# Second projection of a graph-attention layer as seven products of half blocks: six single accumulator banks and three softmax buffers

## The chip, the cores and the metric

The kernel runs on one core of one Trainium2 chip. The metric is the device time of one execution in microseconds.

## The reference

A batch of 32 graphs with 512 nodes and 512 features goes through a layer norm with ReLU and two graph-attention layers, and the input is added at the end. Cut to what matters:

```python
def gat_layer(x, mask, W, a_src, a_dst, bias, concat):
    xl = (x @ W).reshape(B, N, H, F)                   # projection
    e = leaky_relu(asrc[:, :, None, :] + adst[:, None, :, :], 0.2)
    attn = softmax(where(mask, e, -1e9), axis=1)
    out = einsum('bsdh,bshf->bdhf', attn, xl)          # gather
    ...
h = elu(gat_layer(h, mask, W1, ..., b1, concat=True))  # 4 heads of 256
h = gat_layer(h, mask, W2, ..., b2, concat=False)      # 1 head of 512: W2 is 1024 x 512
out = x + h
```

## The kernel before

One loop step works on three batches at once. TensorE's order is written by hand: first projection and first gather of batch i+1, second projection of batch i, second gather of batch i-1. The compiler orders the other engines. The softmax runs on VectorE and ScalarE between these stages; its row terms are transposed by TensorE (`prr`), copied by VectorE (`rrr`), written to DRAM (`drr`) and read back to all partitions (`orr`).

The second projection is plain: 4 tiles of rows, 8 slices of the contraction, two halves of columns, and per tile a pair of banks of PSUM, the memory in which TensorE's sums build up. The two attention columns of W2 ride along, one at each end.

```python
def project2(b):
    h1 = H1.pop(b)
    v = x2(b)
    for t in range(NT):
        ps = psum.tile([P, 2, 512], F32, tag="mm", name=f"pxm{b}_{t}", bufs=3)
        for k in range(FT):
            for j in range(2):
                nc.tensor.matmul(
                    ps[:, j, : W - 1], h1[:, k, t * P : (t + 1) * P],
                    w2_sb[:, k, j * (W - 1) : (j + 1) * (W - 1)],
                    start=(k == 0), stop=(k == FT - 1),
                )
            ...
        nc.scalar.activation(
            v[:, t, :].rearrange("p (c w) -> p c w", c=2), ps[:, :, : W - 1], AF.Copy
        )
```

## Time and profile before

| | before |
|---|---|
| time, median of 3 runs | 3347.83 us (3346.74 to 3349.3) |
| TensorE busy | 3244.2 us, 97% |
| VectorE, ScalarE busy | 64%, 52% |
| TensorE idle: start, middle, tail | 54.4, 26.8, 15.5 us |
| half clock after 215 us and before the tail | none |

The last two rows are sums over the trace: start is the first 215 us, tail the last 165 us (idle time up to TensorE's last matmul), middle what lies between. TensorE's granted clock is recorded in windows: 12 in the trace of this kernel, each at 1.0 or at 0.5 of full clock. A busy TensorE with little idle time means that taking work from it should pay, as long as nothing else comes late.

Two groups of the page that the prediction did not use; columns are operation, operands, count, busy us, mean ns, idle time before:

```profile
L235 DVE CUSTOM_DVE_ANT_0 l<-l,mt 128x512 f32<-128x512 f32 x640 | 532.9, 861 | 499.2 <-ACT l L232 498.2
L360 POOL TENSOR_TENSOR xr<-xr,b_sb 128x1024 f32<-128x1024 f32 x64 | 194.9, 3046 | 2818.6 <-DMA xr<-in_x_dram 2450.4
```

The median of the first group is 690 ns. A mean of 861 says that a few of the 640 are far longer: 55 of them take 2.7 us on average.

### The profile page before, as it was taken

What the parts mean: (1) busy time and instruction counts of PE and PEld (TensorE: products, weight loads), DVE (VectorE), ACT (ScalarE), POOL (GpSimd) and SP (SyncE); (2) the same over time, 40 slices, a digit from 0 to 9 for tenths busy, and PEclk for the clock granted to TensorE, in tenths of its full rate; (3) what the DMA queues carried; (4) which work ended last, traced back from release to release, by engine and by line L of the source; (5) the groups of instructions that cost most, each with busy time, mean ns of one, the idle gap of its engine ahead of it and who ended that gap; (6) DMA issues with size and microseconds to landing.
All of it is one profiled execution on the core that took longest, in us unless ns stands there. A gap on an engine that the chain in (4) does not pass through costs nothing.

```text
span 3345.9 us, 35756 instructions
## 1 busy us (share of the span) xinstructions
PE 3244.2 (97%) x12544; PEld 2221.7 (66%) x12544; DVE 2128.6 (64%) x4675; ACT 1748.3 (52%) x3489; POOL 228.3 (7%) x102
## 2 busy tenths in 40 slices
PE   4999999999999999999999999999999999999997
PEld 3666676676676666776666766766766667667664
DVE  6567666666666566666676665666665766666663
ACT  3555555545555445555455554455554555554551
POOL 0000000000000000000000000000000000000000
PEclk8999999999999999999999999999999999999998
DMA  5112222222222122222122221222221222221111
GB/s 186 46 60 79 92 95 79 70 76 79 92 91 74 63 81 84 95 83 81 62 79 92 95 79 64 83 78 91 91 76 57 82 89 95 80 71 62 67 67 54
DMA packets 120389, 269.41 MB, mean 81 GB/s; under 512 B 15504, under 2 KB 20496, under 8 KB 120208
## 3 DMA queue, kind: packets, MB, share of 16 engines
q1 hardware_dynamic: 120208, 267.12, 23.7%
q8 instruction: 98, 1.61, 0.2%
q14 instruction: 83, 0.68, 0.1%
HBM read 232.53 MB, written 34.54 MB: 80 GB/s over the span
## 4 chain that ended last, share of the span: by engine, by line
PE 67%; DVE 18%; DMA 8%; ACT 4%; issue 1%; POOL 1%; SPq 0%; POOLq 0%; ACTq 0%; DVEq 0%
PE po L301 26%; PE pxl L282 20%; PE pxm L334 10%; PE po L366 9%; DVE p L261 5%; DVE l L235 5%; DVE p L269 3%; DMA oas<-das 2%; DMA x<-in_x_dram 2%; ACT l L232 2%; ACT l L239 2%; DMA orr<-drr 2%; DMA das<-ras 1%; DVE hn L151 1%; DMA adj<-in_adj_dram 1%
## 5 line engine op out<-in xcount | busy, mean ns | idle before, releaser
L282 PE MATMUL pxl<-w_sb,ht 128*128 128x258 f32 x4096 | 933.5, 384 | 2.4 <-DVE j L101 2.4
L334 PE MATMUL pxm<-w_sb,h 128*128 128x257 f32 x4096 | 922.4, 379 | 0.0
L301 PE MATMUL po<-p,xl 128*128 128x512 f32 x2048 | 891.1, 594 | 0.0
L282 PEld LDWEIGHTS pxl<-w_sb,ht 128*128 128x128 f32 x4096 | 768.5, 191 | 126.8 <-issue 11.5
L235 DVE CUSTOM_DVE_ANT_0 l<-l,mt 128x512 f32<-128x512 f32 x640 | 532.9, 861 | 499.2 <-ACT l L232 498.2
L334 PEld LDWEIGHTS pxm<-w_sb,h 128*128 128x128 f32 x4096 | 761.6, 190 | 126.0 <-issue 10.4
L301 PEld LDWEIGHTS po<-p,xl 128*128 128x128 f32 x2048 | 388.0, 191 | 474.2 <-issue 454.6
L265 ACT ACTIVATE p<-p,lo 128x512 f32<-128x512 f32 x640 | 429.2, 716 | 471.0 <-DVE p L261 470.5
L232 ACT ACTIVATE l<-oas,sc 128x512 f32<-128x512 f32 x640 | 427.1, 710 | 211.7 <-DMA oas<-das 211.7
L239 ACT ACTIVATE l<-l,low 128x512 f32<-128x512 f32 x640 | 454.3, 711 | 130.2 <-DVE low L235 129.7
L261 DVE SCALAR_TENSOR_TENSOR p<-orr,lo 128x512 f32<-128x512 f32 x640 | 444.7, 749 | 82.2 <-DMA orr<-drr 82.0
L366 PE MATMUL po<-xl,p 128*128 128x512 f32 x1024 | 459.3, 595 | 14.6 <-DVE p L269 14.6
L269 DVE TENSOR_TENSOR p<-p,m 128x1024 f32<-128x1024 f32 x320 | 385.9, 1224 | 2.9 <-ACT p L265 2.9
L360 POOL TENSOR_TENSOR xr<-xr,b_sb 128x1024 f32<-128x1024 f32 x64 | 194.9, 3046 | 2818.6 <-DMA xr<-in_x_dram 2450.4
L286 ACT ACTIVATE xl<-pxl 128x516 f32<-128x516 f32 x256 | 149.0, 594 | 416.9 <-PE pxl L282 416.6
L366 PEld LDWEIGHTS po<-xl,p 128*128 128x128 f32 x1024 | 188.0, 191 | 225.8 <-issue 223.8
L311 ACT ACTIVATE e<-po,b_sb 128x512 f32<-128x512 f32 x256 | 171.3, 681 | 297.7 <-PE po L301 152.8
L312 DVE TENSOR_SCALAR e<-e 128x512 f32<-128x512 f32 x256 | 108.7, 425 | 172.5 <-ACT e L311 172.1
L313 DVE SCALAR_TENSOR_TENSOR h<-po,b_sb,e 128x512 f32<-128x512 f32 x256 | 192.1, 751 | 14.7
L142 DVE BATCH_NORM_STATS2 stats<-x 128x6 f32<-128x512 f32 x128 | 87.7, 686 | 95.4 <-DMA x<-in_x_dram 94.9
L239 ACT ACTIVATION_READ_ACCUMULATOR l<-l,low 128x1 f32 x640 | 120.5, 188 | 0.0
L180 DVE TENSOR_SCALAR mt<-pm 128x512 bf16<-128x512 bf16 x128 | 53.3, 417 | 104.5 <-PE pm L177 103.8
(43 smaller groups left out, 1066.7 us busy)
## 6 DMA issues: line engine op xcount, KB each, us to landing
orr<-drr SPq DMA_DIRECT2D x160, 512.0 KB
x<-in_x_dram SPq DMA_DIRECT2D x128, 256.0 KB
adj<-in_adj_dram SPq DMA_DIRECT2D x128, 256.0 KB
xr<-in_x_dram SPq DMA_DIRECT2D x128, 256.0 KB
oas<-das SPq DMA_DIRECT2D x64, 512.0 KB
out_dram<-xr SPq DMA_DIRECT2D x128, 256.0 KB
oas<-das SPq DMA_DIRECT2D x32, 256.0 KB
drr<-rrr SPq DMA_DIRECT2D x160, 4.0 KB
```

Of the source, the lines that this page charges most:

```text
L232: nc.scalar.activation(e, self.asr[i][:, j, :], AF.Prelu, bias=ad[:, d : d + 1], alpha=SLOPE)
L235: nc.vector.tensor_tensor_reduce(out=e, in0=e, in1=MASKT[self.b][:, d, :], scale=-1.0, scalar=BIG, op0=OP.add, op1=OP.min, accum_out=low[: ...
L239: nc.scalar.activation(e, e, AF.Exp, bias=low[:, d : d + 1], scale=-1.0, accum_out=tot[:, d : d + 1])
L261: nc.vector.scalar_tensor_tensor(p[:, u, :], rr[:, 0, :], lo[:, 0, j, u : u + 1], rr[:, 1, :], op0=OP.add, op1=OP.max,)
L265: nc.scalar.activation(p[:, u, :], p[:, u, :], AF.Exp, bias=lo[:, 1, j, u : u + 1])
L269: nc.vector.tensor_tensor(pp, pp, MASK[self.b][:, t : t + 2, :], op=OP.min)
L282: nc.tensor.matmul(ps[:, j, :W], ht[:, k, t * P : (t + 1) * P], w1_sb[:, k, hp + j, :], start=(k == 0), stop=(k == KT - 1),)
L301: nc.tensor.matmul(ps[:, f, :], xl[:, s, h, 2 + f * P : 2 + (f + 1) * P], p[:, s, :], start=(s == 0), stop=(s == NT - 1),)
L313: nc.vector.scalar_tensor_tensor(H1[b][:, g, :], ps[:, f, :], bias, e, op0=OP.add, op1=OP.max)
L334: nc.tensor.matmul(ps[:, j, : W - 1], h1[:, k, t * P : (t + 1) * P], w2_sb[:, k, j * (W - 1) : (j + 1) * (W - 1)], start=(k == 0), stop=(k ...
L360: nc.gpsimd.tensor_tensor(xr, xr, b2_sb[:, None, :].to_broadcast([P, 2, D]), op=OP.add)
L366: nc.tensor.matmul(ps[:, j, :], p[:, s, (d + j) * P : (d + j + 1) * P], v[:, s, 1 : DO + 1], start=(s == 0), stop=(s == NT - 1),)
```

## The change

The intent is to save TensorE time. With seven block products in place of eight (the Winograd form of Strassen's scheme), the two halves of rows, contraction and columns need 56 matmuls instead of 64. The price: sums of blocks of h1 (`sums2`) and of W2 (once), an evaluation in which several products build up in one bank and are read in between, and SBUF (on-chip memory) space. So the pairs of banks become six single banks, the softmax weights get three buffers instead of four, the score tiles three instead of four, and the normalised rows overwrite x. The core of the diff, cut:

```diff
-    w2_sb = const.tile([P, FT, DO + 2], F32, name="w2_sb")
+    w2_sb = const.tile([P, 7, KH, W2H], F32, name="w2_sb")
...
-            p = work.tile([P, NT, N], F32, tag="p", name=f"p{self.b}_{self.layer}_{h}", bufs=4)
+            p = work.tile([P, NT, N], F32, tag="p", name=f"p{self.b}_{self.layer}_{h}", bufs=3)
...
+    def sums2(b):
+        ...
+        nc.vector.tensor_add(s1, a21, a22)
+        nc.vector.tensor_sub(a21, a11, a21)
+        nc.vector.tensor_sub(s2, s1, a11)
+        nc.vector.tensor_sub(s4, a12, s2)
+        LEFT[b] = {1: a11, 2: a12, 3: s4, 4: a22, 5: s1, 6: s2, 7: a21}
...
     def project2(b):
+        def product(m, n, acc, first):
+            if first:
+                bank[m, acc] = psum.tile([P, 512], F32, tag="mm", name=f"pxm{b}_{m}{acc}", bufs=6)
+            ps = bank[m, acc]
+            for k in range(KH):
+                nc.tensor.matmul(
+                    ps[:, :W2H], left[n][:, k, m * P : (m + 1) * P], RIGHT[n][:, k, :],
+                    start=(first and k == 0), stop=(k == KH - 1), skip_group_check=True,
+                )
...
+        for m, n in (
+            (0, 1), (0, 2), (0, 5), (1, 1), (0, 6), (1, 2), (1, 5),
+            (0, 7), (1, 6), (0, 3), (1, 7), (0, 4), (1, 3), (1, 4),
+        ):
+            acc = {1: "a", 2: "g", 5: "b", 6: "a", 7: "a", 3: "b", 4: "a"}[n]
+            product(m, n, acc, n in (1, 2, 5))
+            ...
+            if n in (1, 5, 6):      # ScalarE copies the bank out; the bank goes on
+                nc.scalar.activation(block(*to, m), ps, AF.Copy)
+            elif n == 4:
+                nc.scalar.activation(block(1, 0, m), ps, AF.Copy)
+            else:                   # 2, 7, 3: VectorE adds the bank to a block
+                nc.vector.tensor_add(to, ps, to)
...
-            stages.insert(0 if last else 1, project2(i))
+            order = [g2] * 4 + [c2] * 14
+            if last:
+                order = [g2] * 2 + [c2] * 14 + [g2] * 2
```

Bank "a" of row block m takes product 1, is copied out, takes product 6 on top, is copied out, takes 7, is added to a block, and takes 4. Before each of these steps the program makes TensorE wait for the read of the step before (such waits for ScalarE's copies come to 93 us in the profile after). "(1, 7)" below means product 7 of row block 1.

## The prediction

> **What bounds the kernel now.** I read the busy shares first, then the costliest groups, the waits of TensorE, a table by stage, and at last the order of events inside one batch. The busy shares, the granted clock and the costliest TensorE groups of the page:
>
> ```profile
> PE 3244.2 (97%) x12544; PEld 2221.7 (66%) x12544; DVE 2128.6 (64%) x4675; ACT 1748.3 (52%) x3489; POOL 228.3 (7%) x102
> ...
> PEclk8999999999999999999999999999999999999998
> ...
> L282 PE MATMUL pxl<-w_sb,ht 128*128 128x258 f32 x4096 | 933.5, 384 | 2.4 <-DVE j L101 2.4
> L334 PE MATMUL pxm<-w_sb,h 128*128 128x257 f32 x4096 | 922.4, 379 | 0.0
> ```
>
> TensorE is the bound: 97% busy, at full clock after the start. The second projection (L334) has 4096 records for 32 batches, 128 per batch; the code issues 4 x 8 x 2 = 64 matmuls per batch, so each f32 matmul is two records. The mean of 379 ns holds pipeline overlap. The price is the distance of starts, from the TensorE timeline of the second projection of one middle batch:
>
> ```profile
> 1582.68 3.64 PE L334 MATMUL pxm<-w_sb,h 128*128 128x257 f32 x16
> 1586.15 0.60 PE L156 MATMUL pht<-identf,hn 128*128 128x128 f32 x4
> 1586.59 3.64 PE L334 MATMUL pxm<-w_sb,h 128*128 128x257 f32 x16
> 1590.07 0.27 PE L196 MATMUL prr<-identf,r 128*8 128x128 f32 x1
> 1590.18 3.64 PE L334 MATMUL pxm<-w_sb,h 128*128 128x257 f32 x16
> ...
> 1606.04 0.27 PE L196 MATMUL prr<-identf,r 128*8 128x128 f32 x1 [0.79 <-DVE rrr L198]
> ```
>
> 16 records take 1586.15 - 1582.68 = 3.47 us: **217 ns each**. The one steady gap is the last line: the transpose of head 3's row terms waits for a VectorE copy that frees its PSUM buffer. The waits of TensorE over the whole run (columns: total us, times, longest us):
>
> ```profile
> PE prr L196 <- DVE rrr L198: 26.2, 27, 1.8
> PE prr L196 <- DVE r L246: 20.1, 4, 7.3
> PE po L366 <- DVE p L269: 14.6, 1, 14.6
> PE pht L156 <- DVE hn L151: 10.0, 2, 9.4
> ```
>
> The first is the steady gap, 0.8 to 0.9 us per batch; the others are the start and the tail. So TensorE sets the time, but with no room: the softmax chain of VectorE, ScalarE and DMA arrives 0.8 us late per batch. The table by stage of that batch (first projection, second gather, second projection, first gather):
>
> ```profile
> 1539.10:1568.30 29.20, 29.20 (x148) 25.15 (x147) 13.64 (x31) 11.24 (x20) 0.00 (x0) 1.00 0.22 73
> 1568.30:1582.70 14.40, 14.40 (x40) 6.45 (x39) 9.00 (x31) 12.69 (x31) 0.00 (x0) 1.00 0.36 113
> 1582.70:1613.10 30.40, 29.61 (x144) 25.34 (x143) 24.13 (x45) 15.28 (x33) 7.66 (x3) 1.00 0.35 121
> 1613.10:1640.70 27.60, 27.60 (x67) 12.18 (x66) 19.39 (x40) 15.11 (x28) 0.00 (x0) 1.00 0.10 29
> ```
>
> Columns are the stretch, its us, then busy us of PE, weight load, DVE, ACT, POOL. VectorE is at 24.1 of 30.4 us in the second projection and 19.4 of 27.6 in the first gather, but only 13.6 of 29.2 in the first projection.
>
> [...] from 1598.7 to 1602.7 ScalarE idles for VectorE's p while the eviction of a finished projection tile waits behind it.
>
> **The change part by part.**
>
> Removed: a batch goes from 64 to 14 x 4 = 56 matmuls of 257 columns (the attention columns ride along, one in each half). That is 16 records x 217 ns = 3.47 us a batch, **111.1 us** over 32.
>
> Added on VectorE per batch: four sums of 128x1024, about 1.13 us each start to start[...]: 4.5 us. They stand in the first projection, where VectorE has 15 us free, and are needed 14 us of second gather later: hidden. Six additions of a finished product from PSUM, 257 columns, 0.4 us each: 2.4 us, inside the crowded stage. Four gather additions of 512 for two of 1024: +0.4 us. VectorE goes to about 73 of 98 us: still no bound by sum. ScalarE's evictions become half as wide and twice as many: 1 us more at most. Both hidden by sum.
>
> At the start: the attention columns of W2 take 32 reductions of 256 columns at 0.35 us (start distance of L101) instead of 16 of 512 at 0.61 (L116): +1.4; four small adds 0.6; four subtractions of the half blocks of 1028 columns, 4.5. VectorE's queue holds TensorE up there (waits for m and mt), so about **+6 us**. In the first batch the second projection no longer stands in front of its first softmax transposes: the four empty turns of the gather pass at once, about **+5 us**.
>
> At the tail: before, after the last first gather TensorE ran the whole second projection at once (from 3266.97), and only then needed the weights of the batch before, ready at 3277.8. Now two gather steps come first and must wait for these weights: 11 us, up to 15 if the sums get ahead of them, say 13. After the projection the gather that hides the last softmax is half as long, and the rows' transpose comes one gather step later. From the end of the first gather to the last gather: before 3324.6 - 3267 = 57.6 us; after about 13 + 6.9 + 24.3 + 3.4 + 28.6 (the measured way from 3296.0 to 3324.6) = 76.2. That is +18.6, and as the 3.5 us saved are already counted, **+22 us**.
>
> Six single banks for three pairs: the same PSUM. Three softmax buffers for four: head 3's weights wait until head 0's gather ends, 7 us into the first gather; they are needed at 20.6 us and take about 7: hidden. Row normalising in place: hidden.
>
> **The steady term, where I choose.** Before, eviction of a projection tile started on average 2.5, 5.0, 1.0 and 5.0 us after its last matmul (mean over 32 batches, computed from the trace), and it did not matter, since three pairs of banks were there. Now a later product accumulates on the same bank, so TensorE must wait for the read in between. The distance is three products (5.2 us) for block one, two (3.5) for the next, and for the second row block's 6 to 7 only one, 1.7 us; the final reuse of the first bank has 3.5. Also, the transposes of heads 2 and 3 are now three products (5.2 us) apart where they were two half tiles (6.9), and the copy between them is the one that is already late. Against that, the compiler's order of VectorE and ScalarE will be another one, and a stall of TensorE gives the chain time. I take 1.2 us more than the present gap per batch, **+36 us** over 30 batches.
>
> Sum: 3347.8 - 111.1 + 6 + 5 + 22 + 36 = **3306 us**.
>
> **The rivals.** (1) The saving arrives whole but for the ends: steady term zero, 3270 us, or 3245 if the finer banks also close the present gap. For it: VectorE and ScalarE have idle time, and the order of products is interleaved with care. Against: the chain is late already and gets 2.8 us more VectorE work in its stage. (2) A new wait takes the place: evictions behind blocked queue heads stall TensorE about 3 us a batch, giving 3360. For it: latencies of 5 us against distances of 1.7 to 3.5. Against: the compiler orders the evictions anew, and one stall gives the later ones time. (3) VectorE becomes the bound: against it, 73 of 98 us. (4) The DMA queue: 24% of its engines' time, and no transfer grows: no change.
>
> **Range and chances.** A steady term of -0.6 to +2.9 us a batch round 3270 gives 3252 to 3357. Faster by over 2% means under 3281, a steady term under 0.4 us: 0.30. Slower by over 2% means over 3415, a term near 5 us: 0.08. Within 2%: 0.62.
>
> **What would show each step.** The second projection's records should fall to 3584 at an unchanged start distance of 217 ns; otherwise the saving is mis-sized. The waits of TensorE should list the projection's products waiting for ScalarE's copy or VectorE's addition, and the prr wait, together about 2 us a batch; if they total under 0.9, rival one holds, and if over 4, rival two. A wait of 11 to 15 us of the second gather should stand before the last projection, and the last wait for p should be near 22 us; if either is missing the tail term is wrong. A wait of the first product for the sums would show that they are not hidden. The prediction is wrong most easily by the order of the two in-order queues, which I cannot see.

3347.8 - 111.1 + 6 + 5 + 22 + 36 is 3305.7. The 1.13 us of a sum: in the profile before, the next instruction starts 1.135 us after a mask minimum of this size (median of 283). What the profile after shows for the new work of VectorE: 1.20 to 1.23 us for a sum of h1, the four of a batch together 5.4 us where 4.5 were given; 0.40 to 0.42 us for the addition of a product; 2.7 us a batch for the four gather additions, 2.4 for the two before; 1.20 to 1.22 us for each of the four subtractions of 1028 columns.

## More of the kernel before

The line of GpSimd is untouched by the change, and it will matter:

```python
def gather2(b):
    for d in range(0, NT, 2):
        xr = work.tile([P, 2, D], F32, tag="xr", name=f"xr{b}_{d}", bufs=2)
        ...  # two loads of x
        nc.gpsimd.tensor_tensor(xr, xr, b2_sb[:, None, :].to_broadcast([P, 2, D]), op=OP.add)
        ...  # matmuls into ps
        nc.vector.tensor_tensor(xr, ps, xr, op=OP.add)
        ...  # stores
```

In the second gather GpSimd adds the bias to the residual rows ahead of time, and VectorE adds the gathered sum.

## The result and the profile after

| | before | after |
|---|---|---|
| median of four fast runs | 3348.28 us | 3376.72 us (3373.38 to 3383.01) |
| ratio after to before | | 1.0088, interval 1.007 to 1.0105 |
| TensorE matmul records | 12544 | 12032 |
| TensorE busy, profiled run | 3244.2 us | 3184.9 us |
| TensorE idle: start, middle, tail | 54.4, 26.8, 15.5 us | 59.3, 91.6, 31.9 us |
| half-clock windows in the middle | 0 | 22, together 92.2 us |

A ratio is the mean time of one kernel's fast runs over that of the other's of the same rounds, so it is not quite the ratio of the medians. The change made the kernel 0.9% slower, outside the range of 3252 to 3357 us.

The busy shares and the clock of the page after:

```profile
PE 3184.9 (94%) x12032; PEld 2158.0 (64%) x12032; DVE 2324.9 (69%) x5099; ACT 1791.2 (53%) x3873; POOL 218.9 (6%) x102
...
PEclk8899999999999999999999999999999999999998
```

There are exactly 512 records fewer, 32 x 16, and they should take away 111.1 us. TensorE's busy time fell by 59.3 us only; the other 51.8 us are matmuls that ran slower. The strip of the clock hides this, since most half-clock windows in the middle (3.4 us) are short against a slice of 84 us; the mean granted clock shows it, 0.973 after 0.989. The waits of TensorE over the run:

```profile
PE pxm_1a L381 <- ACT xl L399: 88.3, 30, 4.4
PE prr L227 <- DVE r L277: 31.8, 6, 12.0
PE po L427 <- DVE p L300: 19.8, 2, 10.6
```

The 26 us for the transposes are gone. In their place (1, 7) waits for ScalarE's copy of (1, 6) out of their common bank, 2.9 us a time. The TensorE timeline of one batch:

```profile
1494.27 1.90 PE L381 MATMUL pxm_1a<-w_sb,hs 128*128 128x257 f32 x8
1496.01 0.27 PE L227 MATMUL prr<-identf,r 128*8 128x128 f32 x1
1496.11 1.91 PE L381 MATMUL pxm_0b<-w_sb,hs 128*128 128x257 f32 x8
1497.86 0.60 PE L187 MATMUL pht<-identf,x 128*128 128x128 f32 x4
1502.40 3.62 PE L381 MATMUL pxm_1a<-w_sb,h 128*128 128x257 f32 x8 [3.94 <-ACT xl L399]
1505.85 1.90 PE L381 MATMUL pxm_0a<-w_sb,h 128*128 128x257 f32 x8
```

(1, 6) ends at 1496.0. One product stands between, then TensorE idles 3.94 us. And the eight records after the gap take 3.45 us from start to start instead of 1.74: a half-clock window of 3.413 us begins at 1502.3. Over the middle of this trace, a half-clock window began in, or at most 1.3 us after, 20 of 20 gaps of over 2.4 us, 2 of 5 of 1.6 to 2.4 us, and none of 14 of 0.1 to 1.6 us. ScalarE at the same time:

```profile
1497.85 0.37 ACT L399 ACTIVATE xl<-pxm_1b 128x257 f32<-128x257 f32 x1
1501.35 0.72 ACT L296 ACTIVATE p<-p,lo 128x512 f32<-128x512 f32 x1 [3.14 <-DVE p L292]
1501.98 0.36 ACT L399 ACTIVATE xl<-pxm_1a 128x257 f32<-128x257 f32 x1
```

ScalarE is idle for 3.14 us with the copy second in its queue: the exponential ahead of it waits for VectorE. VectorE and GpSimd, in this order:

```profile
1491.47 3.38 DVE L300 TENSOR_TENSOR p<-p,m 128x1024 f32<-128x1024 f32 x1
1494.77 0.27 DVE L229 COPY rrr<-prr 8x128 f32<-8x128 f32 x1
...
1500.57 2.74 DVE L292 SCALAR_TENSOR_TENSOR p<-orr,lo 128x512 f32<-128x512 f32 x4 [1.03 <-DMA orr<-drr]
```

```profile
1490.89 2.87 POOL L422 TENSOR_TENSOR xr<-xr,b_sb 128x1024 f32<-128x1024 f32 x1 [7.92 <-DMA xr<-in_x_dram]
```

So the chain is, backwards: copy of the bank, exponential, head 1's weights, the row terms from DRAM (5.5 us after their copy), the copy `rrr` at 1494.77, and in front of it a mask minimum that takes 3.38 us instead of 1.22, while GpSimd adds the bias.

The trace shows that this is no single case. 45 VectorE instructions take over 2 us: 26 mask minima, 17 score minima (`l`) and 2 of the start. Every one of these 43 minima began while a GpSimd addition was running, and ended 1.08 us (mask) or 0.55 us (score) after that addition's end, just under its usual length. They take 92 us more than at their medians of 1.22 and 0.69 us.

Where the 25.7 us between the profiled runs come from: 111.1 us of records less; idle time up by 64.8 in the middle, 4.9 at the start and 16.4 in the tail; half clock up by 46.1, 1.7 and 7.2 (half the length of the windows in each stretch). That sums to +30, but it counts some time twice: of the half-clock windows 63.1 us lie in idle time, 43.6 before. So about 10 of the 55 us of half clock are no loss: 3 in the middle, 2 at the start, 5 in the tail. Without them, and with the drain after the last matmul 1 us shorter, the sum is +19; some 6 us stay unexplained.

### The profile page after: what moved, and what is told of

Its sections match the earlier page's. It is cut to its first block, busy times and chain, and to the rows that moved or that the text cites. A ratio compares the mean times of both kernels' runs of the same rounds, so it can differ in the third digit from the quotient of the medians.

```text
span 3371.6 us, 35481 instructions
## 1 busy us (share of the span) xinstructions
PE 3184.9 (94%) x12032; PEld 2158.0 (64%) x12032; DVE 2324.9 (69%) x5099; ACT 1791.2 (53%) x3873; POOL 218.9 (6%) x102
## 3 DMA queue, kind: packets, MB, share of 16 engines
q1 hardware_dynamic: 121280, 267.12, 24.7%
## 4 chain that ended last, share of the span: by engine, by line
PE 49%; DMA 19%; ACT 15%; DVE 14%; issue 1%; SPq 0%; POOL 0%; ACTq 0%; DVEq 0%
PE po L333 26%; PE pxl L313 12%; ACT l L263 6%; ACT l L270 6%; DMA oas<-das 6%; DMA orr<-drr 5%; PE pxm_1a L381 5%; DVE p L300 4%; DVE p L292 3%; DVE l L266 3%; DMA adj<-in_adj_dram 3%; PE pxm_0a L381 2%; DMA das<-ras 2%; DMA drr<-rrr 2%; PE pxm_1b L381 2%
## 5 line engine op out<-in xcount | busy, mean ns | idle before, releaser
L266 DVE CUSTOM_DVE_ANT_0 l<-l,mt 128x512 f32<-128x512 f32 x640 | 462.4, 745 | 575.8 <-ACT l L263 573.6
L296 ACT ACTIVATE p<-p,lo 128x512 f32<-128x512 f32 x640 | 436.1, 717 | 250.2 <-DVE p L292 249.3
L317 ACT ACTIVATE xl<-pxl 128x258 f32<-128x258 f32 x512 | 188.7, 381 | 535.7 <-PE pxl L313 535.1
L300 DVE TENSOR_TENSOR p<-p,m 128x1024 f32<-128x1024 f32 x320 | 439.0, 1393 | 1.2 <-ACT p L296 1.1
L422 POOL TENSOR_TENSOR xr<-xr,b_sb 128x1024 f32<-128x1024 f32 x64 | 185.5, 2898 | 2592.4 <-DMA drr<-rrr 1128.2
L381 PE MATMUL pxm_1a<-w_sb,h 128*128 128x257 f32 x768 | 214.9, 428 | 88.3 <-ACT xl L399 88.3
L381 PEld LDWEIGHTS pxm_1a<-w_sb,h 128*128 128x128 f32 x768 | 159.8, 212 | 121.3 <-ACT xl L399 95.4
L381 PE MATMUL pxm_0a<-w_sb,h 128*128 128x257 f32 x768 | 200.3, 406 | 4.5 <-ACT xl L399 4.2
L381 PEld LDWEIGHTS pxm_0a<-w_sb,h 128*128 128x128 f32 x768 | 159.7, 209 | 49.5 <-issue 14.7
L381 PE MATMUL pxm_0b<-w_sb,hs 128*128 128x257 f32 x512 | 121.9, 380 | 0.0
```

The source lines that it names most:

```text
L266: nc.vector.tensor_tensor_reduce(out=e, in0=e, in1=MASKT[self.b][:, d, :], scale=-1.0, scalar=BIG, op0=OP.add, op1=OP.min, accum_out=low[: ...
L296: nc.scalar.activation(p[:, u, :], p[:, u, :], AF.Exp, bias=lo[:, 1, j, u : u + 1])
L300: nc.vector.tensor_tensor(pp, pp, MASK[self.b][:, t : t + 2, :], op=OP.min)
L317: nc.scalar.activation(xl[:, t, h, :], ps[:, :W], AF.Copy)
L381: nc.tensor.matmul(ps[:, :W2H], left[n][:, k, m * P : (m + 1) * P], RIGHT[n][:, k, :], start=(first and k == 0), stop=(k == KH - 1), skip_ ...
```

## The experiments

Twelve kernels ran; "idle" and "windows" are TensorE's idle time and the half-clock windows in the middle of the profiled run. All were correct but e3, which is wrong on purpose. The compiler orders VectorE and ScalarE anew for each kernel, so an edit of TensorE's order can change theirs.

| run | median us | ratio to before | idle us | windows, us |
|---|---|---|---|---|
| after | 3376.7 | 1.0088 | 91.6 | 22, 92 |
| e1_far | 3464.8 | 1.0338 | 160.7 | 29, 177 |
| e2_near | 3478.2 | 1.0381 | 167.7 | 29, 184 |
| e3_nopool | 3265.7 | 0.9741 | 27.7 | 2, 7 |
| e4_eight | 3367.3 | 1.0045 | 28.2 | 3, 10 |
| e8_filler | 3360.2 | 1.0022 | 54.7 | 7, 24 |
| e6_bias | 3260.1 | 0.9730 | 25.0 | 1, 3 |
| e7_turn | 3321.8 | 0.9917 | 51.0 | 9, 41 |
| e5_tail | 3366.4 | 1.0035 | 88.5 | 20, 85 |
| b1_bias_before | 3309.5 | 0.9879 | 1.0 | 0 |
| c1_bias_tail | 3235.4 | 0.9661 | 24.7 | 3, 10 |
| c2_bias_tail_turn | 3238.2 | 0.9668 | 19.9 | 0 |
| c3_bias_tail_far | 3313.9 | 0.9890 | 70.6 | 15, 55 |

### The dose: how far apart the two products stand (e1, e2)

```diff
 # e1_far
-            (0, 1), (0, 2), (0, 5), (1, 1), (0, 6), (1, 2), (1, 5),
-            (0, 7), (1, 6), (0, 3), (1, 7), (0, 4), (1, 3), (1, 4),
+            (0, 1), (0, 2), (0, 5), (1, 1), (0, 6), (1, 2), (1, 5),
+            (1, 6), (0, 7), (0, 3), (1, 7), (0, 4), (1, 3), (1, 4),
 # e2_near
+            (0, 7), (0, 3), (1, 6), (1, 7), (0, 4), (1, 3), (1, 4),
```

> One thing changed against the changed kernel: the order of the fourteen products, so that two products (3.5 us) instead of one (1.7 us) stand between product 6 and product 7 of the second row block, which share a bank. Theory A (TensorE waits for ScalarE's read of that bank, and every such wait of over about 2.4 us also costs 3.4 us at half clock): the wait before product 7 of the second block falls from 88 us in total to under 30, the half-clock windows in the middle nearly vanish, and the time falls by 60 to 110 us, to 3265 to 3315. Rival B (the chain of VectorE, ScalarE and DMA is simply too slow for the shorter TensorE work, so the lost time only moves to another wait): the total of TensorE's waits in the middle stays near 90 us and the time stays within 20 us of 3377.

> The opposite dose: product 7 of the second row block directly follows its product 6, so no product stands between. Theory A: each wait grows by about the 1.7 us taken away, from 2.9 to about 4.6 us on average, all of them now over 2.4 us and so all with a half-clock stretch: 32 x (1.7 + about 0.5) = about +70 us, near 3445. Rival B: no change beyond 20 us.

e2 went the way theory A said, and further: the waits of (1, 7) rose from 88 to 165 us, the time by about 100 us to 3478. But it isn't a pure dose. With its product, the compiler moved ScalarE's copy of (1, 6) too: in 29 batches it stands behind one exponential of head 1's weights in the changed kernel, and behind four in e2. One batch of e2:

```profile
1442.74 2.71 ACT L296 ACTIVATE p<-p,lo 128x512 f32<-128x512 f32 x4 [3.31 <-DVE p L292]
1445.35 0.37 ACT L399 ACTIVATE xl<-pxm_1a 128x257 f32<-128x257 f32 x1
```

The copy starts 2.61 us after the blocked exponential in place of 0.63 (1501.35 to 1501.98 above). These 2.0 us are most of the 2.5 us by which the mean wait in the middle grew. So the place of the copy in ScalarE's queue counts more than the distance between the products.

e1 broke both expectations: 3465 us. Its waits of TensorE:

```profile
PE pxm_0a L381 <- DVE xl L404: 154.2, 30, 6.3
...
PE pxm_1a L381 <- ACT xl L399: 11.4, 18, 2.0
```

The wait that I aimed at is nearly gone, from 88 to 11 us; in 30 batches the copy of (1, 6) now stands in front of head 1's exponentials. But exchanging (1, 6) and (0, 7) put (0, 7) one product later, and now (0, 4) waits for VectorE's addition of (0, 7), 5.1 us a time. In e1's timeline that addition stands behind the four instructions of head 1's weights and two mask minima, 5 us of VectorE's work; in the changed kernel it started at 1499.14, just ahead of them at 1500.57. So TensorE does wait for the read of its bank, as theory A says, but the cure failed: for some 5 us neither queue serves evictions, and the order of products chose which bank met that stretch.

### What makes the queues stand still (e3, e6, b1)

```diff
 # e3_nopool (the bias is missing in the result)
-                nc.gpsimd.tensor_tensor(
-                    xr, xr, b2_sb[:, None, :].to_broadcast([P, 2, D]), op=OP.add
-                )
 # e6_bias, and b1_bias_before on the kernel before
-                nc.gpsimd.tensor_tensor(
+                nc.vector.tensor_tensor(
                     xr, xr, b2_sb[:, None, :].to_broadcast([P, 2, D]), op=OP.add
                 )
```

> The GpSimd addition of the bias to the residual rows is dropped (the result is wrong on purpose: the second bias is missing). Two VectorE instructions per batch take 2.9 and 3.4 us instead of 0.7 and 1.2 while that addition runs. Theory C (these two are why ScalarE's queue stands still when the bank must be read): the long VectorE instructions vanish, head 1's row terms are sent 2 to 4 us earlier, the wait for the bank falls to under 1 us a batch with no half-clock stretch, and the time falls to 3270 to 3310. If the lateness has another cause, such as the distance of TensorE's transposes from their users: the VectorE instructions shorten but the wait stays at 2 us or more and the time stays over 3350.

> The bias addition to the residual rows moves from GpSimd to VectorE (correct result): two more VectorE instructions of 128x1024 per batch, about 2.3 us. Theory C (GpSimd's addition blocks VectorE for 2.2 us twice a batch, and that makes the bank read late): 2.3 us of work in place of 4.4 us of blocking, so the wait for the bank falls from 88 us to 20 to 60 and most half-clock windows go: 3280 to 3330. Rival E (dropping the addition helped because VectorE has less to do, or because GpSimd's use of its queue and of the DMA order went): no gain, 3370 or more.

Without GpSimd's addition no VectorE instruction takes over 2 us, and the time falls to 3265.7 us, a little below the range that I gave. The orders of TensorE, VectorE, ScalarE and the DMA queue in its trace are those of the changed kernel, instruction for instruction, so nothing but GpSimd's addition is gone. In e6 the result is right and VectorE gets more work, not less: two additions of 1.22 and 1.18 us in the batch below. It came out still lower, 3260.1 us, also below the range. The orders of TensorE and of the DMA queue are identical to the changed kernel's, VectorE's is so but for the added instructions; ScalarE's differs by one exchange of neighbours per batch, which is not at the bank read. The same place of a batch in e6:

```profile
1446.67 0.27 DVE L229 COPY rrr<-prr 8x128 f32<-8x128 f32 x1
...
1452.79 2.74 DVE L292 SCALAR_TENSOR_TENSOR p<-orr,lo 128x512 f32<-128x512 f32 x4 [1.02 <-DMA orr<-drr]
```

```profile
1443.35 0.27 PE L227 MATMUL prr<-identf,r 128*8 128x128 f32 x1
...
1454.62 2.01 PE L381 MATMUL pxm_1a<-w_sb,h 128*128 128x257 f32 x8 [1.31 <-ACT xl L399]
```

From the transpose of head 1's row terms to the start of their copy it is 3.3 us here; in the changed kernel it was 6.3 us (1488.50 to 1494.77). The way through DRAM is the same, 5.5 to 5.9 us. The gap shrinks from 3.94 to 1.31 us and the eight records after it take 1.84 us from start to start, nearly full clock. ScalarE still stands still for 3.4 us, waiting for the DMA; TensorE arrives there at the right time. So GpSimd's blocking is not the only cause of the standing still, but it is what took the gap to a length after which the clock fell: 22 half-clock windows in the middle with it, 1 without.

> The kernel before with the same one-word edit: the bias addition on VectorE. Its only steady wait was 26 us for a late VectorE copy, and its banks leave 5 us of slack for evictions. Theory C for the whole case (GpSimd's blocking of VectorE hurts only where TensorE depends closely on evictions): 10 to 28 us faster than before, 3320 to 3340, against 117 us in the changed kernel. Rival (the edit is simply worth some 3% to any version of this kernel, and says nothing of the change): 3230 to 3270.

The same word changed in the kernel before gives 3309.5 us, 41 us less than its 3350.7 of those rounds: more than I expected, and far less than the rival says. Its middle has 1.0 us of idle time left. In the changed kernel the word is worth 117 us. The difference goes with the shared banks, as four kernels show by the idle time of their middle: 91.6 us with shared banks and GpSimd's addition (after), 25.0 with shared banks alone (e6), 28.2 with the addition alone (e4 below, which has 61 VectorE instructions of over 2 us), 1.0 with neither (b1).

### The cost of a gap (e8)

```diff
 # e8_filler
+            if (m, n) == (1, 7):     # bank "g" of row block 0: nobody reads it any more
+                for k in range(KH):
+                    nc.tensor.matmul(
+                        bank[0, "g"][:, :W2H], left[3][:, k, :P], RIGHT[3][:, k, :],
+                        start=(k == 0), stop=(k == KH - 1), skip_group_check=True,
+                    )
             product(m, n, acc, n in (1, 2, 5))
```

> The changed kernel with four useless matmuls (8 records, 1.74 us at full clock) put in front of product 7 of the second row block, where TensorE waits about 3 us a batch. They write a bank that nobody reads any more. Theory A2 (a gap of over about 2.4 us costs 3.4 us of half clock): the gaps shrink to about 1.3 us, the half-clock windows in the middle go (46 us lost to them before), and although TensorE does 14% more work in this stage the kernel gets faster by 20 to 45 us, to 3330 to 3357. Rival (the clock falls for another reason, or costs nothing because TensorE waits anyway): the time rises by 0 to 56 us, to 3377 to 3433.

The kernel does 256 records more and is faster: 3360.2 us against 3376.7 (1.0022 against 1.0088 of before), some 3 us short of the range. Its half-clock windows fell from 22 to 7, 24 us in place of 92. The useless matmuls lie in time that was lost anyway, and with them fewer half-clock windows follow. (The compiler exchanged some VectorE and ScalarE neighbours here too; the copy of (1, 6) still stands behind one exponential.) They are not a good cure; they show that the clock term is real.

How long must a gap be? Over ten runs (after, e1, e2, e3, e5, e6, e7, e8, c1, c3) I counted the gaps of TensorE in the middle and whether a half-clock window began in the gap or within 3.5 us after it: from 1.0 to 1.6 us 0 of 53, from 1.6 to 2.4 us 16 of 46, from 2.4 to 3.2 us 32 of 39, from 3.2 us on 89 of 89. The windows last multiples of 3.413 us (in the run after, 22 windows hold 27 of them), so 3.413 us of half clock full of matmuls cost 1.7 us.

### The rest of the change (e4, e5, e7)

```diff
 # e4_eight: after, with plain products; no sums of h1 or W2
+        for t in range(NT):
+            for c in range(2):
+                ps = psum.tile([P, 512], F32, tag="mm", name=f"pxm{b}_{t}{c}", bufs=6)
+                for k in range(FT):
+                    nc.tensor.matmul(
+                        ps[:, :W2H], h1[:, k, t * P : (t + 1) * P],
+                        AT[k // KH, c][:, k % KH, :],
+                        start=(k == 0), stop=(k == FT - 1),
+                    )
+                    ...  # a yield after every 4 or 5 matmuls
+                nc.scalar.activation(v[:, t, c * W2H : (c + 1) * W2H], ps[:, :W2H], AF.Copy)
 # e5_tail
-                order = [g2] * 2 + [c2] * 14 + [g2] * 2
+                order = [c2] * 14 + [g2] * 4     # softmax of the last batch right after c2
     ...
 # e7_turn
-                    9: lambda: (s1.turn(1), s1.first(3)),
-                    10: lambda: s1.second(1),
+                    7: lambda: (s1.turn(1), s1.first(3)),
+                    8: lambda: s1.second(1),
```

> The changed kernel with its six single banks, three softmax buffers, normalising in place and its order of stages, but with the plain eight products (64 matmuls a batch, no sums, no shared bank). It tells the cost of the rest of the change. Theory A: the rest costs only the start and the tail, about 30 us, less the wait of 26 us for the transposes that no longer shows: 3335 to 3375. Rival D (three buffers, or the six additions less, set the lateness): waits of over 1 us a batch appear elsewhere and the time is over 3390.

3367.3 us, in the range. With all 64 matmuls but no bank read on the way, the single banks, three buffers and the new order cost 0.45%. The tail holds it: idle time and half clock there are 29.7 and 15.4 us against 15.5 and 9.9 before, at most +20 us, since some of the half clock lies in the idle time; the middle is like that of the kernel before, with 28 us of waits for the transposes. Rival D falls.

> Only the last batch differs: its whole second projection comes first and all four gather steps of the batch before it come after, as in the kernel before. My tail term (+22 us, of which the profile shows 16 us of idle time and 7 us of half clock) says 10 to 20 us faster, 3357 to 3367; TensorE then waits some 8 us for the sums of the last batch instead of 10.6 us for the weights, and the gather hides more of the last softmax. If the tail is set by something else, under 5 us.

3366.4 us: 10 us less by the medians, 18 us by the ratios (1.0035 against 1.0088), inside the expectation. In the profiled run, which is the fastest of the four by 16 us and lowers the mean, the idle time of the tail falls from 31.9 to 16.6 us.

> Head 1's row terms are transposed two products earlier (after product 7 of the gather-and-products order instead of 9), so that their way through DRAM starts up to 3.5 us earlier. If the distance from that transpose to its user is what makes VectorE and ScalarE stand still, the wait for the bank falls by 1 to 3 us a batch: 3280 to 3340. If the late VectorE copy behind GpSimd's addition sets it, the landing moves by under 0.5 us and the time stays within 20 us of 3377.

3321.8 us. That is in the first range, but it does not isolate the distance: the new order also changed what GpSimd runs into. Only 25 VectorE instructions took over 2 us instead of 45, and one mask minimum instead of 26. With the bias on VectorE the earlier transpose is worth nothing, as c2 shows.

### Together (c1, c2, c3)

> The changed kernel with the bias addition on VectorE and the last batch reordered as in e5_tail. The two touch different stretches, so their gains should add: 3260 less the 10 to 24 us of the tail, 3236 to 3252.

> As c1_bias_tail, with head 1's transpose two products earlier. About 24 us of waits for the bank remained with the bias on VectorE; an earlier landing takes away up to those: 3215 to 3245. If instead TensorE then waits for the row terms themselves or for another bank, no gain or a loss of up to 20 us: 3240 to 3270.

> As c1_bias_tail, with the order of products of e1_far. There the wait only moved to the other row block, because both queues stood still for about 5 us. With the standing still cut, the theory says that neither block waits long: 3225 to 3260. If the order itself is bad, whatever GpSimd does: waits of over 3 us before product 4 of the first block stay and the time is over 3300.

c1 is the edit of e6 with that of e5: 3235.4 us (3235.16 to 3238.14), 0.9661 of the kernel before, correct. It beats both kernels, and it also beats b1 by 74 us. Its waits of TensorE:

```profile
PE pxm_1a L381 <- ACT xl L399: 26.4, 22, 2.8
PE prr L227 <- DVE r L277: 18.5, 5, 5.4
```

Of the 111 us, then, the seven products keep 74 once the coupling is relieved. The traces of c1 and b1 account for the rest: 24 us of idle time and 5 of half clock in the middle, 8 us at the start, less 2 in the tail; the spans differ by 71.5 us. c2 is the same within noise (3238.2 us): the waits of (1, 7) fall to 10 us, those of the first row block rise to 15. c3 refutes what I expected. The order of e1 is bad even with the bias on VectorE: (0, 4) still waits 71.5 us in total for VectorE's addition, 2.5 us a time. The wait was halved, from 154 us, not removed. In one batch of c3 (0, 7) ends at 1282.0, and VectorE does this:

```profile
1282.66 2.74 DVE L292 SCALAR_TENSOR_TENSOR p<-orr,lo 128x512 f32<-128x512 f32 x4 [1.31 <-DMA orr<-drr]
1285.32 2.35 DVE L300 TENSOR_TENSOR p<-p,m 128x1024 f32<-128x1024 f32 x2
1287.59 0.42 DVE L404 TENSOR_TENSOR xl<-pxm_0a,xl 128x257 f32<-128x257 f32 x1
```

The addition stands behind 5 us of head 1's weights, as in e1. That place is the compiler's choice, and moving GpSimd's work does not change it.

## Why the prediction was wrong

The prediction gave 3306 us and a range up to 3357; the runs gave 3376.7.

- **The saving on TensorE**: right. 512 records less, and the start distance is unchanged: 1.74 us for eight, 217 ns each.
- **The start, +11**: about +5 us measured. Idle time rose by 4.9 us, the first projection of the second batch began 5.2 us later, and the half clock outside idle time did not grow.
- **The tail, +22**: about +19 us measured (16.4 idle, and 2.4 of clock outside idle time). On the prediction's own stretch, from the end of the first gather to the last gather, it is 73.5 us after 57.6, where 76.2 was expected. The wait before the last projection was 10.6 us, where 11 to 15 were expected; the last wait appeared in two parts, 12.0 for the row terms and 9.2 for the weights, where 22 were expected in one. e5 took 18 us back.
- **The sums hidden**: right, no product waits for them. VectorE's load was right too: 73.0 us in the batch whose stages I summed.
- **The present gap at the transposes**: the prediction kept it and added to it. It vanished, 26 us to nothing. A stalled TensorE gives the chain time: in e4, without the stall, the gap is there again with 28 us.
- **The steady term, +36 us, is the step that failed.** The prediction chose "1.2 us more than the present gap per batch". In the middle the idle time rose by 64.8 us and the half clock took another 43 (46.1 less 3 inside waits): together +108 us, about 3.4 us a batch. The place was named rightly: for the second row block's products 6 and 7 it gave a distance of "only one, 1.7 us" against evictions up to 5 us late. The size was wrong twice over. The wait was 2.9 us where about 2.1 in all was assumed. And a term was left out: what a gap does to the clock. In the ten runs counted above, half clock followed 32 of 39 gaps of 2.4 to 3.2 us and all 89 longer ones.
- **The rivals**: rival two, evictions behind blocked queue heads at 3360 us, was the true story, with the same cause and nearly the same stall; it lacked the clock. The sign that the prediction set for it, waits of over 4 us a batch, did not show: the bank waits were 2.8 us a batch. The text set it aside because "the compiler orders the evictions anew" and since one stall gives later ones time. The second was true, but the first stall alone was enough. That the time stayed within 2%, the outcome given most weight, was luck: the saving was used up by a loss three times the one expected.
- **What the prediction did not see at all**: GpSimd's blocking of VectorE. The mean of 861 ns of a group whose median is 690 was in the profile before.

What stays open: the remaining 24 us of waits in c1, and whether an order of the fourteen products, or a hand-written order of VectorE and ScalarE, exists that keeps the reads out from behind head 1's weights. Only three orders of products were tried.

## What to carry to other kernels

Here fewer matmuls paid only once TensorE did not have to wait long for other engines in between. When a bank is read in the middle of an accumulation, count the reader's queue delay (TensorE waited 2.9 us a time here), not its 0.4 us of work, against the distance to the next product. Count a TensorE gap with its aftermath at half clock: in these traces it followed 121 of the 128 gaps of over 2.4 us and 16 of 46 of 1.6 to 2.4, and 3.413 us of it full of matmuls cost 1.7 us. Look for VectorE instructions whose mean is well above their median (861 and 690 ns here): GpSimd may be holding them up, and then moving GpSimd's work to the busier VectorE can be the faster choice, as it was here by 41 and by 117 us. When a stall moves as the order is changed, as in e1, look at the reader's queue: what makes it stand still, and where the compiler has put the read, since that place moves with the product.
